# A graph layer's packed slots moved in four held transfers, and one multiply per chunk moved from VectorE to GpSimd

## The chip, the cores and the metric

The kernel runs on one core of a Trainium2 chip. The metric is the device time of one execution in microseconds (us); lower is better. Three timed runs of the kernel before took 541.56, 544.33 and 547.14 us, median 544.33. The profile is of one more execution, which took 538.86 us; its span from the first to the last instruction is 537.0 us. The engines are named as in the profile: PE is TensorE, DVE is VectorE, ACT is ScalarE, POOL is GpSimd, SP is SyncE (which here only issues transfers).

## What is computed

A graph network layer with a residual and a layer norm, on 6250 nodes with 128 features and 100,000 edges that are sorted by destination:

```python
Xs = X[src]
m_data = Xs @ W_data.T + b_data
m_ctrl = Xs @ W_control.T + b_control
msg = jnp.where((edge_types == 0)[:, None], m_data, m_ctrl)
agg = jax.ops.segment_sum(msg, dst, num_segments=X.shape[0])
out = jax.nn.relu(agg + (X @ W_self.T + b_self))
x = _layernorm(x + out, axis=-1)
```

Every node thus sums one of two products per incoming edge, chosen by the edge's type.

## The kernel before

**Messages.** At the start both products are computed for all nodes and kept in SBUF as `m3`, each number split into three bf16 parts (384 columns), 98 blocks of 128 rows (49 blocks of nodes, two products each). A copy goes to a table in memory.

**Windows and groups.** The destination nodes are cut into 39 windows of 160 nodes; an edge list of 22 x 126 edges covers a window. Windows come in groups: one of 1, one of 2, nine of 4 (`GROUPS`). The code has two phases per group.

**ranks** (from L720) prepares a group, long ahead of its use. It finds for each edge its block of source rows, counts edges of a block with matmuls (`rk`, L823 and L864) and gets by a reduction on DVE (`slot`, L869) the edge's slot among 32 slots of that block. For two chunks of the group's edges (12 and 10 of the 22 columns, 48 and 40 edge columns for a group of 4 windows) DVE then takes three large bf16 steps: `hr` (L893, the one-hot of the slot, 126 x 1536 or 126 x 1280 elements), and twice a multiply into `two` (L899): `hr` times the row within the block (`lo1`), and `hr` times the destination within the window (`to1`). Matmuls on PE (`scatter`, L908) put these numbers into the slots (`vt`); three small DVE steps (L923 to L929) turn them into `vs`, which SP writes to memory as `packed` (L935). GpSimd then makes `to_d` from `vs` (L492), picks out edges that found no slot (`pv`, L955 and L957), and a list of these is made by DVE, GpSimd and PE in turn (`fl`, `n8b`, `pos`, `hr` L992, matmuls L1011), gathered from the table by GpSimd (L1034) and copied by SP into `gl` (L1041).

**sums** (from L1048) does the windows of a group. SP reads a window's packed slots (3136 numbers of 2 bytes) and gives them to all 128 partitions, 784 KB, into `rows`, which has two buffers (L1061). One DVE step compares them with the partition number (L1071), which makes `rows` a one-hot matrix of 32 slots by 98 blocks. Two DVE steps make `hot` from `to_d` (L1079), the one-hot of the destination. Then come 25 steps g: stage 1 (L1093, four matmuls side by side) gathers 128 slots' messages into PSUM, ACT or DVE evicts them to `gs` (L485 and L486), stage 2 (L1110 and L1113) adds them into the window's sum `a`. `close` adds the window's own product, the ReLU, the residual and the layer norm; its last step is on GpSimd (L678).

**What sets the order.** `add` does not issue an instruction; it records an operation with an engine, an assumed duration and a due time. `Plan.run` then plays the whole program in assumed time: on each engine it takes, of the operations that are ready, the one with the earliest due time, and the order so found is the order in which instructions are issued to each engine's queue. Every queue runs in order on the chip. Assumed durations on GpSimd come from `pool(cols, rate)`, 0.4 + cols x rate / 1000 us, on DVE from `dve(cols, rate)`, 0.07 + cols x rate / 1000 us; a signal from DVE is booked with 0.14 us and one from GpSimd with 0.15 us. Ranks are due about 80 us ahead of their sums, so their operations come first wherever they are ready. `vp(on_pool, ...)` records a step on GpSimd or on DVE:

```python
def vp(on_pool, due, cols, fn, r, w, rate=1.04, slow=1.0):

    if on_pool:
        return add("POOL", pool(cols, slow), lambda: fn(G), due, r, w)
    return add("DVE", dve(cols, rate), lambda: fn(V), due, r, w)
```

Before the change, `RP` is 1, so that L1061 makes one transfer for a window; its place on the queue follows from the planned end of the matmuls that free the buffer.

Of the kernel before, what the change touches and what calls it, by code (L numbers as in the profile page):

```python
# [21 lines left out]
P = 128  # L22
D = 128
D3 = 3 * D
# [20 lines left out]
R = 32  # L45
# [42 lines left out]

class Op:
    __slots__ = ("alts", "due", "lat", "deps", "after", "left", "ready", "start", "end", "out",  # L90
                 "index", "engine", "slack", "size")

    def __init__(self, alts, due, lat):
        self.alts, self.due, self.lat, self.slack, self.size = alts, due, lat, 0.0, 0
        self.deps, self.after, self.out = [], [], []


class Plan:
# [5 lines left out]
    FROM = 60.0  # L104
    BEGIN, RATE, LAND = 1.2, 0.28, 0.8

    def __init__(self):
        self.ops, self.rings, self.far = [], {}, set()

    def add(self, engine, dur, fn, due, r=(), w=(), lat=0.0, size=0):  # L110
        alts = engine if isinstance(engine, list) else [(engine, dur, fn)]
        op = Op(alts, due, lat)
        op.index, op.size = len(self.ops), size
        kind = [(i[0] if isinstance(i, tuple) else i).name for i in w] or ["out"]
        if engine == "SP" and due > self.FROM:
            op.slack = self.SLACK.get(kind[0], 0.0)
        self.ops.append(op)
        deps = set()
        for items, writes in ((r, False), (w, True)):
            for item in items:  # L120
                b, key = item if isinstance(item, tuple) else (item, None)
                for k, (ws, rs) in b.keys.items():
                    if key is None or k is None or k == key:
                        deps.update(ws)
                        if writes:
                            deps.update(rs)
                if writes and key is None:
                    b.keys = {}
                ws, rs = b.keys.setdefault(key, ([], []))
                if writes:  # L130
                    b.keys[key] = ([op], [])
                else:
                    rs.append(op)
                if not b.users or b.users[-1] is not op:
                    b.users.append(op)
        deps.discard(op)
        op.deps = list(deps)
        return op

    def since(self, op, engine):  # L140
        return op.ready + (0.0 if op.alts[0][0] == engine else self.OTHER)

    def run(self):
# [70 lines left out]
                    offer(o)  # L214
                    o.left = -1
        order.sort(key=lambda x: x[:2])
        for _, _, _, fn in order:
            fn()
        return order


# [45 lines left out]
def sums_over_windows(ctx, tc, x, xt, edges, w, bias, out, total):  # L267
# [4 lines left out]
    work = ctx.enter_context(tc.tile_pool(name="work", bufs=2))  # L272
    ps = ctx.enter_context(tc.tile_pool(name="ps", bufs=1, space=PSUM))
    ctx.enter_context(tc.manual_schedule())
    plan = Plan()
    add = plan.add

    table = dram.tile([NT * P, D3], BF16, name="table")
# [15 lines left out]
    GC = 1.3  # L294
    SPD = 0.45
    AD = 0.45
    RP, RA, RS = 1, 14, 0.9
    GAP, LEAD, LF, SF = -12, 80, .3, .010


# [230 lines left out]
    for q in range(NS):  # L531
# [42 lines left out]
        if q % 2 or q == NS - 1:  # L574
# [2 lines left out]
                tv[:, t0:t1, :], m3.t[:, t0:t1, :]), due + 8, m3_key(q) + m3_key(q - q % 2),  # L577
                [(table_b, q)], size=(ts.stop - t0) * P * D3 * 2)


    def own(o, lhs, n):

# [146 lines left out]
    def ranks(gi, w0, nw, when, late, step, engines):  # L729
# [145 lines left out]
        for ci, (k0, k1) in enumerate(zip(cs, cs[1:])):  # L875
# [22 lines left out]
            for i, f in enumerate((lo1, to1)):  # L898
                tf = lambda e, c=c, s4=s4, v4=v4, i=i, f=f, hr=hr, two=two: e.tensor_tensor(  # L899
                    v4(two.t[:EP, :, i, :]), v4(hr.t),  # L900
                    fl(f)[:, c, None, :].to_broadcast(s4), op=ALU.mult)
                vec(dc, m * R, lambda tf=tf: tf(V), [hr, f], [(two, i)], 0.52)

            def scatter(k0=k0, k1=k1, two=two):
                for k in range(k0, k1):
# [144 lines left out]
    def sums(gi, w0, nw, placed):  # L1050
# [5 lines left out]
        for i in range(nw):  # L1056
            due = T0 + (w0 + i) * TW
            sp = B(work, [P, R, NT], BF16, "rows", 2, R * NT)
            for j in range(RP):
                Q = ("ACT", AD, A) if gi < 3 and i == 0 else ("SP", SPD, S)  # L1060
                add(*Q[:2], lambda i=i, sp=sp, j=j, Q=Q: Q[2].dma_start(  # L1061
                    sp.t[P // RP * j : P // RP * (j + 1)].rearrange("p r c -> p (r c)"),
                    packed[gi, i // 2, (i % 2) * 64 : (i % 2) * 64 + R, :]
                    .rearrange("r c -> (r c)")[None, :].to_broadcast([P // RP, R * NT])),
                    due - RA + RS * j, [(packed_b, gi)], [(sp, ("p", j))],
                    size=P // RP * R * NT * 2)
            cut = 2 if gi < 3 else 1
            half = R // cut
            for q in range(cut):
# [16 lines left out]
            for g in range(NS):  # L1086
                d = due + TW * g / NS
                gp = B(ps, [P, 512], F32, *(("g", 3) if gi < 2 or g % 4 < 3 else ("x", 1)))
                last = g == NS - 1

                def stage1(g=g, gp=gp, sp=sp, last=last):
                    for t in (0, 1) if last else turn(4, D3):
                        T.matmul(gp.t[R * t : R * t + R, :D3], sp.t[:, :, 4 * g + t],  # L1093
                                 m3.t[:, 4 * g + t, :], start=True, stop=True)
                s1.append(add("PE", 0.163, stage1, d, [sp] + m3_key(g), [gp]))
                lag = 2 if gi < 2 else 3
                if g >= lag:
                    s2[g - lag].after.append(s1[g])
                if last:
                    gs = gls[i]  # L1100
                    evict(lambda gs=gs: gs.t[:64], lambda gp=gp: gp.t[:64, :D3], D3, d + 0.3,
                          [gp], [(gs, "t")], LAT)
                else:
                    gs = B(work, [P, D3], BF16, "gs", 6)
                    evict(lambda gs=gs: gs.t, lambda gp=gp: gp.t[:, :D3], D3, d + 0.3, [gp], [gs],
                          LAT)

                def stage2(g=g, gs=gs, a=a, hot2=hot2, last=last):
                    for j in turn(4, D3):
                        T.matmul(a.t[R * j : R * j + R, :D3], hot2.t[:, g, R * j : R * j + R],  # L1110
                                 gs.t, start=g == 0, stop=False, skip_group_check=True)
                    for c, j in enumerate(turn(3, D, [3] * (g == 1))):
                        T.matmul(a.t[R * j : R * j + R, D3:], hot2.t[:, g, P:],  # L1113
                                 gs.t[:, c * D : (c + 1) * D], start=False, stop=g > 0,
                                 skip_group_check=True)
                s2.append(add("PE", 0.204, stage2, d + 0.9, [gs, (hot2, sum(g >= c for c in cuts[1:-1]))], [a]))
                s2[-1].slack = .1
                if g == 12:
                    def own_a(i=i, a=a, xc=xc):
                        own(lambda j, m: a.t[R * j : R * j + R, :D],  # L1120
                            lambda j, m: xc.t[:, i * WN + R * j : i * WN + R * j + R], P)
                    add("PE", 0.28, own_a, d + 1, [xc, w_sb, one3, brows], [a])
            bs = B(work, [P, D], F32, "bs", 5)
            evict(lambda bs=bs: bs.t, lambda a=a: a.t[:, D3:], D, due + TW + 0.8, [a], [bs]).slack = 0.25
            got.append((w0 + i, a, due + TW + 0.8, bs))
        return got

# [264 lines left out]
```

## Time and profile before

| | |
|---|---|
| timed runs, us | 541.56, 544.33, 547.14 |
| profiled execution, us | 538.86 |
| its span, us | 537.0 |
| mean granted TensorE clock | 0.987 |
| bytes moved, MB | 63.03, mean 117 GB/s |
| transfers of packed slots | 36 from SP, 3 from ACT, 784 KB each |
| rate of the 16 DMA engines' busy time from 260 to 460 us | 0.35 |

How to read the lines below. A line of the timeline has the start in us after the span's start, the duration in us, engine, line of the kernel, operation, output from input, and in brackets the idle time of the engine just before it and what ended it. A line of groups has the shape, the count, then the busy time in us, the mean in ns, and the idle time before them. A line of waits has who waited, for whom, then total us, times, and the longest in us. A line of a table by stages has the stage, its length, and for PE, PEld (weight loads), DVE, ACT and POOL the busy time and the number of instructions, then the granted clock, the share of the DMA engines' time and GB/s. "issue" is time in which an engine waited for nothing that the profile shows. A line of the chain has the start, the duration and the work. SPq and POOLq are the queues' own waits and issues.

### The profile page before, as it was taken

To read this page: it belongs to the slowest core of one execution; us is meant where nothing else is said; L and a number is where in the kernel's file an instruction comes from. 1 tells how busy PE (TensorE), PEld (TensorE's weight loads), DVE (VectorE), ACT (ScalarE), POOL (GpSimd) and SP (SyncE) were. 2 spreads that over 40 slices of the span, in tenths; PEclk is the share of its full clock that TensorE was granted. 3 is DMA by queue.
4 is the path that set the end of the run, shared out by engine and by line. 5 is a ranking of instruction groups with operands and counts; after the bars stand their busy time and mean duration, and the time that the engine had idled before them with its cause. 6 is when DMAs were issued, how large, how long until landed. Compare 5 with 4: busy or idle time off the path is not lost.

```text
span 537.0 us, 30923 instructions
## 1 busy us (share of the span) xinstructions
PE 496.3 (92%) x13288; PEld 427.5 (80%) x13288; DVE 434.2 (81%) x1154; ACT 436.0 (81%) x1092; POOL 196.1 (37%) x284
## 2 busy tenths in 40 slices
PE   8999678899999999999998989899899999999991
PEld 5666457799899899989977878888888887899890
DVE  6689798999999999999988979978785796644632
ACT  4687457799898898899888879888887887999991
POOL 1000503501830792564465258375215415402000
PEclk9999899999999999999999999999999999999997
DMA  7576550333343236234324433423332335322300
GB/s 239 194 290 253 170 170 16 110 103 118 90 116 107 78 118 182 76 94 128 100 84 121 137 100 99 137 69 91 99 113 76 95 95 177 114 78 102 121 18 17
DMA packets 44568, 63.03 MB, mean 117 GB/s; under 512 B 18832, under 2 KB 34933, under 8 KB 44405
## 3 DMA queue, kind: packets, MB, share of 16 engines
q1 hardware_dynamic: 41657, 55.90, 32.6%
q0 software_dynamic: 1120, 2.23, 1.8%
q10 hardware_dynamic: 1646, 2.84, 1.5%
q8 instruction: 106, 1.74, 1.3%
q14 instruction: 39, 0.32, 0.2%
HBM read 45.46 MB, written 13.57 MB: 110 GB/s over the span
## 4 chain that ended last, share of the span: by engine, by line
PE 60%; DVE 5%; issue 3%; POOL 2%; ACT 2%; another core or an unknown queue 0%; DVEq 0%; ACTq 0%; POOLq 0%
PE a L1110 22%; PE g L1093 20%; PE x L1093 6%; PE a L1113 4%; PE rk L864 3%; PE vt L908 2%; ACT gs L485 2%; PE a L585 1%; POOL to_d L492 1%; DVE hots L812 1%; PE vt L1011 1%; DVE hot L1079 0%; POOL pv L955 0%; PE rk L823 0%
## 5 line engine op out<-in xcount | busy, mean ns | idle before, releaser
L1110 PE MATMUL a<-gs,hot 128*32 128x384 bf16 x3744 | 359.7, 328 | 1.4 <-ACT gs L485 1.0
L485 ACT CAST gs<-g 128x384 bf16<-128x384 f32 x698 | 303.6, 512 | 56.2 <-PE g L1093 46.1
L1093 PE MATMUL g<-m,rows 128*32 128x384 bf16 x2958 | 302.2, 333 | 8.6 <-DVE rows L1071 3.9
L1093 PEld LDWEIGHTS <-rows 128*32 128x32 bf16 x3822 | 260.0, 134 | 25.7 <-issue 13.2
L1113 PE MATMUL a<-gs,hot 128*32 128x128 bf16 x2808 | 267.4, 220 | 7.1 <-issue 6.9
L1110 PEld LDWEIGHTS <-hot 128*32 128x32 bf16 x3900 | 180.4, 98 | 9.4 <-issue 3.5
L1113 PEld LDWEIGHTS <-hot 128*32 128x32 bf16 x2925 | 152.0, 97 | 19.5 <-issue 10.2
L485 ACT CAST gs<-x 128x384 bf16<-128x384 f32 x212 | 110.0, 519 | 8.4 <-PE x L1093 5.3
L1093 PE MATMUL x<-m,rows 128*32 128x384 bf16 x864 | 94.6, 329 | 1.7 <-ACT gs L485 1.1
L1079 DVE TENSOR_TENSOR hot<-iota_b,to_d 128x1920 bf16<-128x1920 bf16 (+2 forms) x85 | 94.3, 1112 | 0.1
L678 POOL TENSOR_SCALAR xr<-xr,mv,rstd 128x128 f32<-128x128 f32 (+1 forms) x44 | 57.2, 1307 | 42.5 <-DVE rstd L655 39.1
L869 DVE TENSOR_REDUCE slot<-rk 126x8 f32<-126x400 f32 (+2 forms) x99 | 56.1, 567 | 14.7 <-PE rk L864 12.3
L628 DVE TENSOR_REDUCE s<-a 128x128 f32<-128x384 f32 (+1 forms) x40 | 22.0, 551 | 32.2 <-PE a L1113 21.3
L1071 DVE TENSOR_SCALAR rows<-rows,pid 128x3136 bf16<-128x3136 bf16 (+1 forms) x46 | 41.8, 908 | 2.2 <-DMA rows<-packed 2.2
L823 PE MATMUL rk<-hots,later 126*32 126x200 bf16 (+1 forms) x210 | 43.1, 246 | 0.3 <-DVE hots L816 0.3
L864 PE MATMUL rk<-hots,tri 128*32 128x400 bf16 (+1 forms) x388 | 41.2, 334 | 1.5 <-DVE slot L869 1.5
L492 POOL COPY to_d<-vs 32x100 bf16<-32x100 bf16 (+1 forms) x72 | 34.9, 485 | 10.8 <-issue 4.8
L955 POOL TENSOR_SCALAR pv<-slot 126x88 f32<-126x88 bf16 x9 | 10.7, 1188 | 73.3 <-DVE slot L886 73.3
L1034 POOL DMA_INDIRECT sr<-table,at x20 | 23.6, 1178 | 17.5 <-DVE slot L886 11.0
L816 DVE TENSOR_TENSOR hots<-hots,val 126x1200 bf16<-126x1200 bf16 (+3 forms) x42 | 28.0, 672 | 0.0
L812 DVE TENSOR_TENSOR hots<-iota_b,st 126x1200 bf16<-126x1200 bf16 (+3 forms) x42 | 28.0, 675 | 0.1
L864 PEld LDWEIGHTS <-tri 128*32 128x32 bf16 x428 | 20.9, 96 | 6.1 <-issue 4.7
(227 smaller groups left out, 648.7 us busy)
## 6 DMA issues: line engine op xcount, KB each, us to landing
rows<-packed SPq DMA_DIRECT2D x36, 784.0 KB
table<-m SPq DMA_DIRECT2D x12, 768.0 KB
xc<-in_xt SPq DMA_DIRECT2D x9, 320.0 KB
rows<-packed ACTq DMA_DIRECT2D x3, 784.0 KB
xr<-in_x SPq DMA_DIRECT2D x8, 256.0 KB
out<-xr SPq DMA_DIRECT2D x8, 256.0 KB
gl<-sr SPq DMA_DIRECT2D x39, 48.0 KB
rows<-in_xt SPq DMA_DIRECT2D x5, 256.0 KB
```

Of the source, the lines that this page charges most:

```text
L485: [("ACT", act(cols), lambda: A.copy(o(), src())), ("DVE", dve(cols), lambda: V.tensor_copy(o(), src()))], None, None, due, r, w, lat)
L492: "POOL", 0.25 + cols * 0.0014, lambda: G.tensor_copy(o(), src()), due, r, w)
L678: fp = lambda k=k, m=m: G.tensor_scalar(h.t[:m, k, :], h.t[:m, k, :], mv.t[:m, k, 0:1], rstd.t[:m, k : k + 1], op0=ALU.subtract, op1=ALU.mult)
L812: vec(when + 2 + pace * k0, m * NC, lambda k0=k0, k1=k1, hs4=hs4, hp=hp: V.tensor_tensor(hp(), iota1_b.t[:EP, :NC].rearrange("p (c d) -> p ...
L823: T.matmul(cnt.t[3 * R :, :wide], later.t[:EP, R - 1 - k : 2 * R - 1 - k], flat(k, k + 1, EP), start=k < 1, stop=k > KT - 3, skip_group_ch ...
L864: T.matmul(acc.t[R * j : R * j + R, : (k1 - k0) * wide], tri.t[:, R * j : R * j + R], flat(k0, k1, P), start=True, stop=True, skip_group_c ...
L869: vec(due, (k1 - k0) * wide, lambda k0=k0, k1=k1, acc=acc: V.tensor_reduce(slot.t[:, k0:k1, :], acc.t[:EP, : (k1 - k0) * wide].rearrange(" ...
L1071: add("DVE", dve(half * NT, 0.305) + 0.05, lambda sp=sp, rs=rs: V.tensor_scalar(sp.t[:, rs], sp.t[:, rs], pid1.t, None, op0=ALU.is_equal), ...
L1079: lambda i=i, hot2=hot2, s4=s4, c0=c0, c1=c1: V.tensor_tensor(hot2.t[:, c0:c1].rearrange("p g (c d) -> p g c d", d=2), iota1_b.t.rearrange ...
L1093: T.matmul(gp.t[R * t : R * t + R, :D3], sp.t[:, :, 4 * g + t], m3.t[:, 4 * g + t, :], start=True, stop=True)
L1110: T.matmul(a.t[R * j : R * j + R, :D3], hot2.t[:, g, R * j : R * j + R], gs.t, start=g == 0, stop=False, skip_group_check=True)
L1113: T.matmul(a.t[R * j : R * j + R, D3:], hot2.t[:, g, P:], gs.t[:, c * D : (c + 1) * D], start=False, stop=g > 0, skip_group_check=True)
```

## The change

Two things change.

1. The transfer of a window's packed slots. From the fourth group on (32 windows) it becomes four transfers of 32 partitions each, 196 KB. The first is due as before (14 us ahead of the window's due time), the others 0.5 us apart behind it; each of the others is held until stage 1 of the window before has done its step g = 3, 6 or 9: the planner counts this matmul among the transfer's dependencies, and a wait on its signal is added to the transfer. For this, an operation keeps its gate and its instruction, `stage1` returns its last matmul, and `marks` keeps every window's stage-1 operations. The first three groups keep one transfer.

2. The second multiply into `two` (with `to1`) goes to GpSimd from the fourth group on, with an assumed duration of 0.4 us + 2.2 ns a column; in the first three groups it stays on DVE.

```diff
+    def hold(self, op, gate):
+
+        op.gate = gate
+        op.deps.append(gate)
...
-        for _, _, _, fn in order:
-            fn()
+        for _, _, op, fn in order:
+            op.inst = fn()
+            if op.gate is not None:
+                self.tc.add_manual_dep(
+                    op.inst.ins, op.gate.inst.ins.name, mybir.DependencyInfo(
+                        mybir.DependencyClass.Sync, mybir.DependencyReason.SCHED_ONLY),
+                    reason="spread transfers")
...
-    RP, RA, RS = 1, 14, 0.9
+    RP, RA, RS = 4, 14, 0.5
...
-                vec(dc, m * R, lambda tf=tf: tf(V), [hr, f], [(two, i)], 0.52)
+                vp(i == 1 and gi >= 3, dc, m * R, tf, [hr, f], [(two, i)], 0.52, 2.2)
...
-            for j in range(RP):
+            gate = marks[w0 + i - 1] if gi >= 3 else None
+            cut = RP if gate else 1
+            for j in range(cut):
                 Q = ("ACT", AD, A) if gi < 3 and i == 0 else ("SP", SPD, S)
-                add(*Q[:2], lambda i=i, sp=sp, j=j, Q=Q: Q[2].dma_start(
-                    sp.t[P // RP * j : P // RP * (j + 1)].rearrange("p r c -> p (r c)"),
+                op = add(*Q[:2], lambda i=i, sp=sp, j=j, Q=Q, cut=cut: Q[2].dma_start(
+                    sp.t[P // cut * j : P // cut * (j + 1)].rearrange("p r c -> p (r c)"),
                     packed[gi, i // 2, (i % 2) * 64 : (i % 2) * 64 + R, :]
-                    .rearrange("r c -> (r c)")[None, :].to_broadcast([P // RP, R * NT])),
+                    .rearrange("r c -> (r c)")[None, :].to_broadcast([P // cut, R * NT])),
                     due - RA + RS * j, [(packed_b, gi)], [(sp, ("p", j))],
-                    size=P // RP * R * NT * 2)
+                    size=P // cut * R * NT * 2)
+                if j:
+                    plan.hold(op, gate[3 * j])
...
                 def stage1(g=g, gp=gp, sp=sp, last=last):
                     for t in (0, 1) if last else turn(4, D3):
-                        T.matmul(gp.t[R * t : R * t + R, :D3], sp.t[:, :, 4 * g + t],
-                                 m3.t[:, 4 * g + t, :], start=True, stop=True)
+                        mm = T.matmul(gp.t[R * t : R * t + R, :D3], sp.t[:, :, 4 * g + t],
+                                      m3.t[:, 4 * g + t, :], start=True, stop=True)
+                    return mm
...
+            marks.append(s1)
```

Since the planner knows the new durations and waits, the order on all queues is worked out anew.

More of the change, by code (lines that the diff above doesn't have):

```diff
@@ L90 @@
     __slots__ = ("alts", "due", "lat", "deps", "after", "left", "ready", "start", "end", "out",
-                 "index", "engine", "slack", "size")
+                 "index", "engine", "slack", "size", "gate", "inst")
     def __init__(self, alts, due, lat):
@@ L95, in __init__ @@
         self.deps, self.after, self.out = [], [], []
+        self.gate, self.inst = None, None
 class Plan:
@@ L105, with __init__ @@
     BEGIN, RATE, LAND = 1.2, 0.28, 0.8
-    def __init__(self):
+    def __init__(self, tc):
+        self.tc = tc
         self.ops, self.rings, self.far = [], {}, set()
@@ L274, in sums_over_windows @@
     ctx.enter_context(tc.manual_schedule())
-    plan = Plan()
+    plan = Plan(tc)
     add = plan.add
@@ L578, in sums_over_windows @@
                 [(table_b, q)], size=(ts.stop - t0) * P * D3 * 2)
+    marks = []
     def own(o, lhs, n):
```

## The prediction

> **What bounds the kernel now.** I read the page first, then busy time by stage, then what each engine waits for, then single stretches of the timeline.
>
> ```profile
> span 537.0 us, 30923 instructions
> PE 496.3 (92%) x13288; PEld 427.5 (80%) x13288; DVE 434.2 (81%) x1154; ACT 436.0 (81%) x1092; POOL 196.1 (37%) x284
> PE 60%; DVE 5%; issue 3%; POOL 2%; ACT 2%; another core or an unknown queue 0%; DVEq 0%; ACTq 0%; POOLq 0%
> q8 instruction: 106, 1.74, 1.3%
> ```
>
> PE carries 60% of the chain that ended last and "issue" 3%. The table of stages (per stage: PE busy, its instructions, then PEld, DVE, ACT, POOL) says where PE is not full:
>
> ```profile
> 110.00:260.00 150.00, 148.94 (x4477) 136.49 (x4473) 142.75 (x346) 134.45 (x345) 66.45 (x94) 1.00 0.37 114
> 260.00:460.00 200.00, 186.25 (x5508) 165.25 (x5502) 167.04 (x414) 166.37 (x424) 93.99 (x132) 1.00 0.35 104
> 460.00:520.00 60.00, 59.88 (x1765) 53.84 (x1760) 30.30 (x64) 58.48 (x156) 9.22 (x10) 1.00 0.27 89
> ```
>
> From 110 to 260 and from 460 on PE has no room (1.1 and 0.1 us idle). From 260 to 460 it idles 13.75 us: what the change can win lies there. PE's waits from 110 to 520 (in total, times, longest):
>
> ```profile
> PE a L1113 <- issue: 6.9, 8, 2.2
> PE vt L1011 <- DVE hr L992: 2.4, 2, 2.0
> PE g L1093 <- issue: 0.8, 3, 0.3
> PE x L1093 <- issue: 0.5, 1, 0.5
> ```
>
> 8.2 us (6.9 + 0.8 + 0.5) of PE's idle time is "issue": no semaphore held it. Two rows show one such stop, in the middle of a straight run of matmuls; the SP queue's rows and the DMA table (last column GB/s) show what went on:
>
> ```profile
> 347.49 0.22 PE L1113 MATMUL a<-gs,hot 128*32 128x128 bf16 x1
> 349.89 0.23 PE L1113 MATMUL a<-gs,hot 128*32 128x128 bf16 x2 [2.17 <-issue]
> ```
>
> ```profile
> 342.39 0.35 SPq L1061 DMA_DIRECT2D rows<-packed  x1
> 342.80 0.43 SPq L1053 DMA_DIRECT2D xc<-in_xt  x1
> 343.40 0.38 SPq L601 DMA_DIRECT2D xr<-in_x  x1
> ```
>
> ```profile
> 344.50:346.50 2.00, 2.00 (x82) 1.85 (x80) 2.00 (x4) 1.16 (x5) 0.00 (x0) 1.00 0.94 318
> 346.50:347.70 1.20, 1.20 (x36) 0.88 (x28) 1.20 (x2) 1.20 (x5) 0.00 (x0) 1.00 0.99 313
> 347.70:349.90 2.20, 0.03 (x8) 0.01 (x4) 1.26 (x3) 0.45 (x2) 0.00 (x0) 1.00 0.20 51
> ```
>
> The packed slots and what SP issues right behind them saturate the DMA engines until 347.7; PE stops there and comes back 2.2 us later. The instruction queue of the page moved 1.74 MB in 106 packets, 16.4 KB each; PE and PEld ran 26,576 instructions, 251 a packet. So PE lives on pages of about 250 instructions, one per 4.3 us (3,525 instructions in the last 60 us stage are 58.8 per us). A page asked for during a burst of 4 to 5 us comes too late. The chain has two more such stops:
>
> ```profile
> 286.72 1.49 issue
> 385.51 1.45 issue
> ```
>
> The second comes 5.4 us after a transfer of packed slots (380.15, below). This is my reading; no row names the fetch.
>
> **The change, part by part.**
>
> 1. *The transfer in four.* From the fourth group on (32 of 39 windows) the 784 KB of a window become 4 x 196 KB; the first goes as before, the others wait on SP for stage-1 matmuls 3, 6 and 9 of the window before. Removed: the burst. The largest load at once falls from 784 + 320 + 256 KB to 196 + 320 + 256 KB, at some 310 GB/s from 4.4 to 2.5 us, well under the 4.3 that a page lasts. Of the 8.2 us I take off 7.3 (low end 0, if the stops have another cause; high end 8.2).
> [...]
>
> Added: 96 issues on SP of 0.35 us and three waits per window. SP already stands there:
>
> ```profile
> SPq L1061 <- PE g L1093: 187.3, 32, 11.2
> 380.15 0.33 SPq L1061 DMA_DIRECT2D rows<-packed  x1
> 392.20 0.34 SPq L1061 DMA_DIRECT2D rows<-packed  x1
> 386.01 1.03 DVE L1071 TENSOR_SCALAR rows<-rows,pid 128x3136 bf16<-128x3136 bf16 x1
> ```
>
> A window lasts 12.05 us (392.20 - 380.15), so matmul 9 of 25 comes 4.3 us in; with 0.3 us for the issue and, as an estimate, 2.5 us to land (196 KB at 310 GB/s is 0.6; the 1360 KB issued from 342.39 on were through at 347.7, 0.9 us more than the 4.4 they take at 310 GB/s; I allow 1 more), the last quarter is there at 387.3 instead of before 386.01. The compare (1.03 us) can still end 3.8 us before 392.2. Queued behind the waiting SP are the counts of the ranks (past), the list rows (gl), xr and out; the planner knows of the waits and orders SP by them, and for these transfers ranks, matmuls and closing steps would wait. I cost this at 0; if the compare comes after the window's start, PE waits for all that is late, in each of 32 windows.
>
> 2. *The multiply moved to GpSimd.* 16 steps (two chunks in each of 8 groups) leave DVE:
>
> ```profile
> L899 DVE TENSOR_TENSOR two<-hr,to 126x1280 bf16<-126x1280 bf16 x9 | 9.4, 1046 | 0.0
> L899 DVE TENSOR_TENSOR two<-hr,to 126x1536 bf16<-126x1536 bf16 x9 | 8.8, 972 | 0.0
> ```
>
> 8 x (1.05 + 0.97) = 16.1 us of DVE. PE hardly waits for DVE: 2.4 us at L1011 above is the largest, so the gain is between 0 and 2.4; I take 1.
>
> The price on GpSimd: no row has a two-operand step of this size. The nearest are two small ones (ns min/median/max):
>
> ```profile
> L986 POOL TENSOR_TENSOR pos<-iota_f,pos_all x9: 265/266/1248, 98.4 to 450.1; 126x48 bf16<-126x48 f32 x9
> L783 POOL TENSOR_TENSOR pay<-pay,lof x9: 368/495/1461, 55.7 to 355.8; 126x88 f32<-126x88 f32 x9
> L783 POOL TENSOR_TENSOR pay<-pay,lof 126x88 f32<-126x88 f32 x9 | 6.4, 716 | 0.6
> ```
>
> The last row has the mean, 716 ns. From the minima: (368 - 265) / 40 = 2.6 ns an element and 0.14 us fixed; that makes 4.1 us for 1536 elements and 3.5 us for 1280. The maxima come from DVE:
>
> ```profile
> 408.57 1.25 POOL L986 TENSOR_TENSOR pos<-iota_f,pos_all 126x48 bf16<-126x48 f32 x1
> 408.55 1.15 DVE L1079 TENSOR_TENSOR hot<-iota_b,to_d 128x1920 bf16<-128x1920 bf16 x1
> 409.86 0.98 DVE L992 TENSOR_TENSOR hr<-iota_b,pos 126x1536 bf16<-126x1536 bf16 x1 [0.16 <-POOL pos L986]
> ```
>
> While DVE runs one of its bf16 passes GpSimd stands still: 0.27 us of work took 1.25. Over its nine runs L783 takes 1.9 times its minimum (716 to 368).
>
> The planner books 0.4 + 2.2 ns an element, 3.78 and 3.22 us, and puts the scatter matmuls on PE that far behind. PE runs in order, so what GpSimd takes beyond this, PE waits for; PE now comes some 0.7 us after the last weights (392.75 to 393.47 below), of which I count 0.4 as spare. Walk through the tenth group's two chunks:
>
> ```profile
> 388.96 0.96 DVE L893 TENSOR_TENSOR hr<-slot_f,slot 126x1536 bf16<-126x1536 bf16 x1
> 390.94 0.95 DVE L899 TENSOR_TENSOR two<-hr,lo 126x1536 bf16<-126x1536 bf16 x1
> 391.80 0.95 DVE L899 TENSOR_TENSOR two<-hr,to 126x1536 bf16<-126x1536 bf16 x1
> 393.47 0.88 PE vt L908 x48
> 394.58 1.23 DVE L1079 TENSOR_TENSOR hot<-iota_b,to_d 128x2080 bf16<-128x2080 bf16 x1
> 399.69 0.82 DVE L893 TENSOR_TENSOR hr<-slot_f,slot 126x1280 bf16<-126x1280 bf16 x1
> 400.99 0.79 POOL L957 TENSOR_TENSOR pv<-pv,pay 126x88 f32<-126x88 f32 x1
> ```
>
> First chunk: GpSimd could start at 390.0, does 0.9 us until 390.94, little beside lo, 2.7 until the bf16 pass at 394.58, and ends near 395. Booked is 389.92 + 3.78 and 0.29 for two signals, 394.0, with the spare 394.4: 0.6 us late. Second chunk: GpSimd is busy with pv to 401.78, then 3.5 us, end 405.3; booked 400.51 + 3.22 + 0.29, with the spare 404.4: 0.9 late. 1.5 us a group, 8 groups, 12 us. At the planner's 2.2 ns the steps end 0.5 us earlier, 0.1 and 0.4 late, 4 us in all. Slowed as L783 is, 7.8 and 6.7 us long, they are 3.6 and 3.1 late, 54 us; half of that, 27, is my upper bound, since the stretch above shows DVE between its bf16 passes for more than half of the time. The lower bound is 0. Between 4 and 12 I take 5: a slope from 0.10 us of difference is coarse, and DVE has 1 us less to do beside each step. What stands on GpSimd behind the second chunk (the list) comes later too, but of 3.2 us of that the plan knows.
>
> Sum on the profiled execution (538.86 us, span 537.0): -7.3 - 1 + 5 = -3.3, 535.6 us. That execution was faster than all three timed runs (541.56 to 547.14, median 544.33), so I put the difference on the median: **541.0 us**. About 1% (5.4 us) is what a measurement of this kernel can tell from no change.
>
> **The rivals.**
>
> *GpSimd's step is covered.* If it runs at the planner's rate and DVE's bf16 passes fall elsewhere, it ends within what is booked and the spare; -7.3 - 1.7 (between 1 and 2.4), 535.3 us. For: the bare time is nearly the booked one. Against: lo and the pass at 394.58 stand in the stretch above.
>
> *PE stands at the scatter.* Slower: at L908, in order, PE waits for GpSimd's last weights. From 8.3 / 16 = 0.5 us a chunk beyond the spare on, it eats all that is won. At 1.25 us a chunk PE loses 20 us, less 8.3: 556 us. For: where GpSimd's pos is late today, DVE's L992 waits for it and PE for L992 (2.4 us above). Against: the booked time leaves over half of the step covered in any case.
>
> *Another cause of the stops.* If PE isn't short of pages, the held transfers do nothing: -1 + 5, 548.3 us. For: no row names the fetch. Against: the stop at 347.7 begins when the burst ends, and nothing else ends there. [...]
>
> **How the numbers follow.** The forecast (541, own range 535.5 to 546.5) gets 0.45, the covered step 0.25, the standing PE 0.22, the other cause 0.08. Faster by over 1% (under 538.9): 0.25 and 0.10 of the forecast's; within 1%: 0.35 of the forecast's and 0.03 of the last; slower: 0.22 and 0.05. The range, 530 to 555, takes in the covered step with the whole of 8.2 and 2.4 (533.7; the timed runs lie up to 2.8 off their median) and a PE that stands up to 1.2 us beyond the spare at each scatter.
>
> **What would show it.** Right: PE's waits for "issue" from 110 to 520 under 2 us, none over 1; no DMA stretch of 4 us at over 0.9; L899 on POOL at 4 to 6 us; 0 to 1 us of PE waiting at L908 per chunk. Wrong: issue stops that stay (no fetch behind a burst); L899 on POOL at 7 us or more with PE waits at L908 over 15 us in all; DVE waiting for the rows' transfer.

## The result and the profile after

The changed kernel takes 563.01 us (median of 6 runs, 559.68 to 565.84) where the kernel before takes 541.51 us on the same chip: the ratio is 1.040, with a 95% interval of 1.034 to 1.047. It is slower by 4%; the forecast was 541 us and its range ended at 555.

The page of the profiled execution after: the span, the busy times, and the shares of the chain that ended last.

```profile
span 564.3 us, 31221 instructions
PE 501.9 (89%) x13288; PEld 429.4 (76%) x13288; DVE 459.7 (81%) x1147; ACT 434.6 (77%) x1083; POOL 232.4 (41%) x300
PE 51%; DVE 25%; DMA 8%; POOL 6%; issue 5%; ACT 3%; ACTq 0%; SPq 0%; DVEq 0%; POOLq 0%
```

DVE's share of the chain went from 5% to 25%, and DVE is busy for 25.5 us more than before (459.7 against 434.2), though 16.1 us of work were taken off it. So about 41.6 us (25.5 + 16.1) came onto DVE from somewhere. GpSimd's new step is the next row to look at: by source line (durations as minimum, median and maximum in ns), and by form with the mean.

```profile
L913 POOL TENSOR_TENSOR two<-hr,to x16: 2339/2784/2947, 124.1 to 465.4; 126x1536 bf16<-126x1536 bf16 x8, 126x1280 bf16<-126x1280 bf16 x8
```

```profile
L913 DVE TENSOR_TENSOR two<-hr,lo 126x1536 bf16<-126x1536 bf16 x9 | 27.6, 3062 | 0.0
L913 POOL TENSOR_TENSOR two<-hr,to 126x1280 bf16<-126x1280 bf16 x8 | 22.9, 2858 | 0.0
L913 POOL TENSOR_TENSOR two<-hr,to 126x1536 bf16<-126x1536 bf16 x8 | 22.2, 2780 | 54.1 <-DVE hr L907 40.9 <-PE g L1111 7.7 <-PE x L1111 5.6
```

GpSimd's 16 steps take 45.1 us (22.9 + 22.2), 2.8 us each, less than I had priced. But DVE's multiply with lo, 0.95 us before, has a mean of 3.06 us. The timeline of DVE and GpSimd shows why:

```profile
170.20 1.03 DVE L1089 TENSOR_SCALAR rows<-rows,pid 128x3136 bf16<-128x3136 bf16 x1 [3.23 <-DMA rows<-packed]
...
172.20 0.95 DVE L907 TENSOR_TENSOR hr<-slot_f,slot 126x1536 bf16<-126x1536 bf16 x1
173.55 3.34 DVE L913 TENSOR_TENSOR two<-hr,lo 126x1536 bf16<-126x1536 bf16 x1
176.81 0.55 DVE L642 TENSOR_REDUCE s<-a 128x128 f32<-128x384 f32 x1
177.28 0.56 DVE L883 TENSOR_REDUCE slot<-rk 126x8 f32<-126x400 f32 x1
```

```profile
173.30 2.78 POOL L913 TENSOR_TENSOR two<-hr,to 126x1536 bf16<-126x1536 bf16 x1 [5.58 <-PE x L1111]
```

GpSimd begins at 173.30 and runs its bare time, to 176.08. DVE begins lo 0.25 us later, at 173.55, and ends at 176.89: the 2.53 us that GpSimd still needs, and then its own 0.81. The step that began first was served, and the other stood for the whole rest of it. In the second chunk, here that of an earlier group, DVE begins first:

```profile
128.81 0.90 DVE L1097 TENSOR_TENSOR hot<-iota_b,to_d 128x1440 bf16<-128x1440 bf16 x1
...
135.33 0.81 DVE L913 TENSOR_TENSOR two<-hr,lo 126x1280 bf16<-126x1280 bf16 x1
136.86 2.25 DVE L1097 TENSOR_TENSOR hot<-iota_b,to_d 128x1440 bf16<-128x1440 bf16 x1
```

```profile
135.42 2.93 POOL L913 TENSOR_TENSOR two<-hr,to 126x1280 bf16<-126x1280 bf16 x1
```

There lo is undisturbed, GpSimd takes 2.93 us instead of 2.34, and the next bf16 pass of DVE that follows (hot, 0.90 us at 128.81) takes 2.25. In four other chunks the step that stands is a small one in f32, `inside`, 2.0 us instead of 0.24; before and after by form:

```profile
L753 DVE SCALAR_TENSOR_TENSOR inside<-rel,low 126x88 f32<-126x88 f32 x9 | 2.4, 262 | 0.0
```

```profile
L767 DVE SCALAR_TENSOR_TENSOR inside<-rel,low 126x88 f32<-126x88 f32 x9 | 9.6, 1062 | 0.0
```

So it is not bf16 passes alone that are held. Of the 41.6 us, 30 lie beside GpSimd's steps: 18.9 at lo, 7.2 at `inside`, 3.9 at hot. Another 4.4 us are eight evictions of PSUM that the new order gives to DVE instead of ACT (30 against 22). The other 7 us I have not placed.

What is behind DVE's standing is the loop of ranks. The chain that ended last, around the same place:

```profile
165.26 4.75 DMA rows<-packed
170.20 1.03 DVE rows L1089
...
173.55 0.67 DVE two L913
174.32 2.50 issue
176.81 0.55 DVE s L642
177.36 0.49 DVE slot L883
177.89 0.35 PE rk L878 x4
```

The reduction of the ranks (slot, L883) stands behind lo in DVE's order, and PE's next rank matmuls need it. The 2.50 us called "issue" are the time in which lo stands: no semaphore holds it. PE's waits from 110 to 500 us (total, times, longest):

```profile
PE rk L878 <- DVE slot L883: 10.9, 6, 2.1
PE g L1111 <- DVE rows L1089: 3.8, 3, 1.7
PE vt L1025 <- DVE hr L1006: 3.7, 3, 1.9
...
PE a L1132 <- issue: 1.0, 3, 0.4
...
PE g L1111 <- issue: 0.5, 2, 0.3
...
PE a L1129 <- issue: 0.3, 1, 0.3
```

The waits for "issue" did fall, from 8.2 to 1.8 us. In their place stand 10.9 us for slot, which was no row of PE's before, and 3.8 for rows. The row of the stage from 110 to 260 (PE's busy time first) shows it:

```profile
110.00:260.00 150.00, 136.40 (x4020) 123.07 (x4017) 138.37 (x313) 122.47 (x311) 79.80 (x98) 1.00 0.38 99
```

From 110 to 260 PE had 1.1 us idle before and has 13.6 now, in a stage where it did 4477 matmuls and now does 4020.

### The profile page after: what moved, and what is told of

Same layout as the page of the kernel before. It is cut to its first block, busy times and chain, and to the rows that moved or that the text cites. A ratio compares the mean times of both kernels' runs of the same rounds, so it can differ in the third digit from the quotient of the medians.

```text
span 564.3 us, 31221 instructions
## 1 busy us (share of the span) xinstructions
PE 501.9 (89%) x13288; PEld 429.4 (76%) x13288; DVE 459.7 (81%) x1147; ACT 434.6 (77%) x1083; POOL 232.4 (41%) x300
## 4 chain that ended last, share of the span: by engine, by line
PE 51%; DVE 25%; DMA 8%; POOL 6%; issue 5%; ACT 3%; ACTq 0%; SPq 0%; DVEq 0%; POOLq 0%
PE a L1129 16%; PE g L1111 16%; PE x L1111 4%; DVE two L913 4%; DVE hot L1097 4%; DVE slot L883 3%; PE a L1132 3%; POOL to_d L504 3%; DMA rows<-packed 3%; DVE rows L1089 3%; PE rk L878 3%; ACT gs L497 2%; DVE hr L907 2%; PE vt L922 2%; PE g L561 2%
## 5 line engine op out<-in xcount | busy, mean ns | idle before, releaser
L497 ACT CAST gs<-g 128x384 bf16<-128x384 f32 x690 | 299.6, 504 | 75.4 <-PE g L1111 65.8
L1111 PEld LDWEIGHTS <-rows 128*32 128x32 bf16 x3822 | 256.6, 135 | 33.5 <-issue 12.9
L1132 PE MATMUL a<-gs,hot 128*32 128x128 bf16 x2808 | 259.4, 220 | 1.3 <-issue 1.0
L1129 PEld LDWEIGHTS <-hot 128*32 128x32 bf16 x3900 | 172.7, 98 | 8.9 <-issue 3.7
L1132 PEld LDWEIGHTS <-hot 128*32 128x32 bf16 x2925 | 146.0, 97 | 14.0 <-issue 2.9
L497 ACT CAST gs<-x 128x384 bf16<-128x384 f32 x212 | 107.7, 508 | 14.9 <-PE x L1111 13.8
L1097 DVE TENSOR_TENSOR hot<-iota_b,to_d 128x1920 bf16<-128x1920 bf16 (+2 forms) x85 | 98.2, 1160 | 0.1
L1111 PE MATMUL x<-m,rows 128*32 128x384 bf16 x864 | 91.7, 331 | 1.4 <-ACT gs L497 1.1
L883 DVE TENSOR_REDUCE slot<-rk 126x8 f32<-126x400 f32 (+2 forms) x99 | 56.1, 567 | 14.1 <-PE rk L878 11.5
L692 POOL TENSOR_SCALAR xr<-xr,mv,rstd 128x128 f32<-128x128 f32 (+1 forms) x44 | 50.7, 1160 | 40.7 <-DVE rstd L669 40.4
L913 POOL TENSOR_TENSOR two<-hr,to 126x1536 bf16<-126x1536 bf16 (+1 forms) x16 | 45.1, 2819 | 54.1 <-DVE hr L907 40.9
L878 PE MATMUL rk<-hots,tri 128*32 128x400 bf16 (+1 forms) x388 | 40.5, 337 | 13.4 <-DVE slot L883 12.4
L878 PEld LDWEIGHTS <-tri 128*32 128x32 bf16 x428 | 21.3, 96 | 21.7 <-issue 20.2
L913 DVE TENSOR_TENSOR two<-hr,lo 126x1536 bf16<-126x1536 bf16 (+4 forms) x21 | 36.5, 1738 | 0.0
```

Of the source, the lines that this page charges most:

```text
L497: [("ACT", act(cols), lambda: A.copy(o(), src())), ("DVE", dve(cols), lambda: V.tensor_copy(o(), src()))], None, None, due, r, w, lat)
L692: fp = lambda k=k, m=m: G.tensor_scalar(h.t[:m, k, :], h.t[:m, k, :], mv.t[:m, k, 0:1], rstd.t[:m, k : k + 1], op0=ALU.subtract, op1=ALU.mult)
L878: T.matmul(acc.t[R * j : R * j + R, : (k1 - k0) * wide], tri.t[:, R * j : R * j + R], flat(k0, k1, P), start=True, stop=True, skip_group_c ...
L883: vec(due, (k1 - k0) * wide, lambda k0=k0, k1=k1, acc=acc: V.tensor_reduce(slot.t[:, k0:k1, :], acc.t[:EP, : (k1 - k0) * wide].rearrange(" ...
L1097: lambda i=i, hot2=hot2, s4=s4, c0=c0, c1=c1: V.tensor_tensor(hot2.t[:, c0:c1].rearrange("p g (c d) -> p g c d", d=2), iota1_b.t.rearrange ...
L1111: mm = T.matmul(gp.t[R * t : R * t + R, :D3], sp.t[:, :, 4 * g + t], m3.t[:, 4 * g + t, :], start=True, stop=True)
```

## The experiments

Each result is the ratio to the kernel before on the same chip, with its 95% interval in brackets. Each profile is of one execution.

Theory A (the expectations call it the port theory; the runs show who stands and for how long, not what in the chip makes it so): GpSimd's step and DVE's passes over SBUF exclude each other, and what DVE loses reaches PE by slot. Rivals: the planner's new order costs the time; the transfers in quarters do; PE waits for GpSimd's result.

**Each half alone.** First only GpSimd's step, the transfers whole:

```diff
-    RP, RA, RS = 4, 14, 0.5
+    RP, RA, RS = 1, 14, 0.5
```

> Only the multiply goes to GpSimd; one transfer of 784 KB per window as before. Port theory (a two-operand step on GpSimd and one on DVE exclude each other for the whole length of the one that began first): DVE's multiply with lo still takes 3.3 us beside the 2.8 us step, PE waits some 2 us for the ranks' slots in each of 8 groups, time 552 to 558. Transfer theory (the held quarters land late and that is the loss): time within 1% of before, 536 to 547, though the multiply with lo may be long.

Measured: 1.031 [1.025, 1.037], and the same wait of PE:

```profile
PE rk L878 <- DVE slot L883: 10.4, 8, 2.1
```

Then only the held quarters, both multiplies on DVE:

```diff
-                vp(i == 1 and gi >= 3, dc, m * R, tf, [hr, f], [(two, i)], 0.52, 2.2)
+                vec(dc, m * R, lambda tf=tf: tf(V), [hr, f], [(two, i)], 0.52)
```

> Only the transfers change: four quarters, held at matmuls 3, 6 and 9; both multiplies on DVE. Port theory: the loss of the whole change is mostly gone, time 538 to 548, the rows' compare still waits for its quarters (some 8 us in all). Transfer theory: 555 or more. If PE's unexplained stops were late instruction pages, its waits for issue at the last matmuls of stage 2 (6.9 us before) stay at 1 us as in the changed kernel.

Measured: 1.012 [1.006, 1.018]. The two halves, 17.5 and 6.1 us, add up to the 21.5 us of the whole within their uncertainty.

**GpSimd's multiply in four pieces**, each a quarter of the columns:

```diff
+                    for c0 in range(0, m, cn):
...
+                        add("POOL", pool(m * R, 2.2) / 4, tq, dc, [hr, f], [(two, 1)])
```

> As with GpSimd only (one transfer of 784 KB), but GpSimd's multiply is cut into four steps of a quarter of the columns. Port theory: each step holds DVE for 0.7 us at most, the multiply with lo takes 1.4 to 1.7 us instead of 3.3, the time falls by 5 to 10 us against the uncut step. If DVE is held for another reason (the tile that both read), the multiply with lo stays near 3 us and the time too.

Measured: 1.019 [1.013, 1.025]. By form:

```profile
L919 POOL TENSOR_TENSOR two<-hr,to 126x384 bf16<-126x384 bf16 x32 | 36.5, 1170 | 54.2 <-DVE hr L907 40.7 <-PE g L1121 13.5
L919 POOL TENSOR_TENSOR two<-hr,to 126x320 bf16<-126x320 bf16 x32 | 30.3, 974 | 0.0
...
L913 DVE TENSOR_TENSOR two<-hr,lo 126x1536 bf16<-126x1536 bf16 x9 | 11.3, 1254 | 0.0
```

DVE's lo now stands for no more than a part of one piece (mean 1.25 us, longest 1.50), and PE's wait for slot falls from 10.4 to 3.1 us. GpSimd's steps grew together to 66.8 us (36.5 + 30.3), and still the kernel is faster than with one long step: it is DVE's standing that costs.

**The step kept, its length taken away, the order unchanged.** This run has the instructions of the first one in the same order on every engine; GpSimd's multiply takes 32 columns instead of 1536 or 1280. It leaves out the factor with the destination for the other columns, where `hr` stands in its place.

```diff
-                v4(hr.t),
+                v4(two.t[:EP, :, 1, :] if gi >= 3 else hr.t),
...
+                if gi >= 3:
+                    take = 1 if i else m
```

> The kernel with GpSimd's step and whole transfers (ratio 1.031, DVE's lo at 3.3 us in most chunks), in the same order of instructions on every engine, but GpSimd's multiply takes 32 of the 1536 (1280) elements. Left out: the factor with the destination for the others; hr stands in its place in the weights, so the sums of the wrong lists come out. Port theory (the two steps exclude each other for as long as GpSimd's lasts): lo is back at 0.8 to 1.0 us, PE's wait for slot at L878 under 5 us in all, time within 1.5% of before. Rival (the planner's new order costs the time, not the collision): ratio still 1.025 to 1.035.

Measured: 1.001 [0.997, 1.005], PE's wait for slot 0.9 us. GpSimd's step and lo:

```profile
L918 DVE TENSOR_TENSOR two<-two,lo x16: 806/916/960, 122.6 to 433.1; 126x1536 bf16<-126x1536 bf16 x8, 126x1280 bf16<-126x1280 bf16 x8
L918 POOL TENSOR_TENSOR two<-two,to x16: 235/239/900, 123.7 to 434.1; 126x32 bf16<-126x32 bf16 x16
```

This settles the first half: with the order as it is and the long step gone, all of the 3.1% is gone. The order is thus not its cause. The short step also ends earlier, so this run alone doesn't exclude that PE waits for GpSimd's result. The other profiles do: PE's waits of the changed kernel and of the first run have no row for `two` from GpSimd, and with the four pieces, whose steps are longer in all, that row is 0.3 us. The run also shows that the best that the move could have brought in this order is nothing: here DVE is rid of the 16 us and nearly nobody does them, and the time is that of before.

**GpSimd later, and with one operand.** Three runs tried to move or shrink the collision. In the first only the planner was told that the step needs lo:

```diff
+                vp(i == 1 and gi >= 3, dc, m * R, tf, [hr, f] + [(two, 0)] * (i == 1 and gi >= 3), [(two, i)], 0.52, 2.2)
```

> GpSimd only (one transfer), but GpSimd's multiply begins when DVE's multiply with lo is done. Port theory: the multiply with lo takes 0.95 us again, the collision moves to what DVE does next with two operands in SBUF (hot, 1.2 us, takes up to 3), time 548 to 557, between the uncut step (+17 us) and none. If it is not the overlap of the two that costs, the time stays at 556 to 562.

Measured: 1.050 [1.044, 1.056]. It tested nothing but another order: on the chip GpSimd still began as soon as hr was there, and lo of 1536 columns still took 2.8 us in the mean. The next run put a real wait on lo there, and has the order of this one on DVE, GpSimd and SP:

```diff
+                if i == 1 and gi >= 3:
+                    plan.hold(op, lo_op)
+                lo_op = op
```

> What the run in which GpSimd's multiply was to begin after DVE's multiply with lo was meant to be: there only the planner knew of it and on the chip GpSimd began with the one-hot as before; here GpSimd waits for lo on the chip. Port theory: lo takes 0.95 us in every chunk, the collision moves to the next step of DVE with two operands in SBUF, 1 to 2.5 us longer in some chunks; the time is 1 to 2.5% over before, under the uncut step's 3.1%.

Measured: 1.048 [1.044, 1.052], more than expected. All lo are back at 0.95 and 0.82 us, and the next pass over SBUF stands in their place:

```profile
178.53 2.78 POOL L913 TENSOR_TENSOR two<-hr,to 126x1536 bf16<-126x1536 bf16 x1 [6.08 <-DVE two L913]
```

```profile
178.78 3.36 DVE L1092 TENSOR_SCALAR rows<-rows,pid 128x3136 bf16<-128x3136 bf16 x1
```

That pass is the compare of the rows, with one tensor operand: 3.36 us instead of 1.03, once more the 2.53 us that GpSimd still needs and 0.83 of its own. The next reduction of the ranks stands behind it, and PE's waits for slot are 8.7 us. In this order PE also waits 2.1 us for GpSimd's weights. Why this order costs more than the first run's 3.1%, with the collision at lo or behind it, is open. In the third, GpSimd's step has one operand, in the first run's order; it copies `hr` and leaves out the factor with the destination:

```diff
+                    tf = lambda e, hr=hr, two=two: e.tensor_single_scalar(
+                        two.t[:EP, :, 1, :], hr.t, 1.0, op=ALU.mult)
```

> GpSimd only (one transfer), but its step reads one operand: it copies the one-hot of the slot times 1.0 and leaves out the factor with the destination, so the sums are those of wrong lists. If only a two-operand step on GpSimd holds DVE, the multiply with lo takes 0.95 us again and the time is 536 to 545 on a chip where before is 535 to 542. If any GpSimd step on SBUF holds DVE's two-operand steps, lo takes 0.8 us and what is left of GpSimd's step (1.5 to 2 us), 2.3 to 2.8 in all, and the time is 1 to 2% over before.

Measured: 1.047 [1.043, 1.051]. The step got longer with one operand, not shorter, and lo stands as before:

```profile
L917 POOL TENSOR_SCALAR two<-hr 126x1536 bf16<-126x1536 bf16 x8 | 33.4, 4174 | 54.1 <-DVE hr L907 29.2 <-PE g L1114 24.9
L917 POOL TENSOR_SCALAR two<-hr 126x1280 bf16<-126x1280 bf16 x8 | 29.8, 3727 | 0.6
...
L913 DVE TENSOR_TENSOR two<-hr,lo 126x1536 bf16<-126x1536 bf16 x9 | 27.7, 3074 | 0.0
```

So on neither side is a second tensor operand needed for the collision. With the run above this gives three lengths of GpSimd's step in one order: a short one costs nothing, 44.5 us in all cost 3.1%, 63.2 us (33.4 + 29.8) cost 4.7%.

**The quarters.** Four runs on what the transfers in parts cost. Without the waits:

```diff
-                if j:
-                    plan.hold(op, gate[3 * j])
```

> Four quarters at the same due times, but none is held; both multiplies on DVE. If late instruction pages come from the size of one transfer, the waits for issue stay at 1 us and the time is 533 to 541; if they come from the bytes in flight at once, the stops are back (6 us or more) and the time is that of before, 539 to 545. If the hold costs nothing, this is no faster than the held quarters.

Measured: 1.013 [1.008, 1.018], as with the waits; PE's waits for "issue" are 7.8 us without the waits and 4.1 with them. Two halves, the second held:

```diff
-    RP, RA, RS = 4, 14, 0.5
+    RP, RA, RS = 2, 14, 0.5
...
-                    plan.hold(op, gate[3 * j])
+                    plan.hold(op, gate[5 * j])
```

> Transfers alone, two halves of 392 KB, the second held at matmul 5 of the window before; both multiplies on DVE. If stops come from bytes in flight, PE's waits for issue fall to 2 to 4 us; packets of 64 partitions take 0.30 to 0.35 us; time 538 to 546.

Measured: 1.009 [1.006, 1.013], with 6.3 us of waits for "issue", more than expected. Then the order of before, and the four quarters issued back to back; and the same with quarters of the columns, so that each goes to all 128 partitions:

```diff
+                    for k in range(cut):
+                        Q[2].dma_start(
+                            sp.t[P // cut * k : P // cut * (k + 1)].rearrange("p r c -> p (r c)"),
```

> The kernel before with its order kept: where it issued one transfer of 784 KB, from the fourth group on it issues four of 196 KB one behind the other. If quarters by themselves cost (each takes the DMA engines longer, 0.37 to 0.40 us a packet against 0.29), the time is that of the unheld quarters, 546 to 552, and the compare waits for them 6 us or more; if the new order was the cost, the time is within 0.5% of before. Unexplained stops of PE: 6 us or more in either case, as the bytes in flight are the same.

```diff
+                            sp.t[:, h * k : h * (k + 1)].rearrange("p r c -> p (r c)"),
```

> The kernel before with its order kept; each window's transfer is cut in four along the columns, 8 of the 32 slots each, to all 128 partitions. If the quarters of 32 partitions cost because they reach few partitions at a time, this costs nothing, 0 to 0.5% over before or a little under it; if four transfers instead of one are the cost (issues on SP, pieces under way at the same time), it is 1% over before like the quarters by partitions.

Measured: 1.011 [1.008, 1.015] and 1.017 [1.014, 1.021], with 4.2 and 10.8 us of waits for "issue". The first of these holds nothing and yet has no more of them than the held quarters; I had expected 6 us or more. So that the holds are what lessens the stops is not shown. DVE's waits for the rows from 110 to 545, in the kernel before, with quarters of the partitions, and with quarters of the columns:

```profile
DVE rows L1071 <- DMA rows<-packed: 2.2, 3, 1.5
```

```profile
DVE rows L1074 <- DMA rows<-packed: 14.3, 13, 1.9
```

```profile
DVE rows L1075 <- DMA rows<-packed: 8.0, 10, 2.1
```

So cutting the transfer costs 1% or more without any new order, and it comes later to the compare. The stage of 260 to 460 has the DMA engines busier for the same bytes where the partitions are cut (0.46 against 0.35 before, at 106 and 104 GB/s):

```profile
260.00:460.00 200.00, 188.86 (x5623) 170.10 (x5615) 169.47 (x417) 170.91 (x435) 93.86 (x135) 0.99 0.46 106
```

By columns the share is 0.36, and that run is no faster; the busier engines are not the whole cause, and the rest stays open. One run changed the order alone, by a planner's cost (0.5 us for an issue on SP):

```diff
-    SPD = 0.45
+    SPD = 0.5
```

> The kernel before with one assumed duration in the planner changed (an issue on SP 0.5 instead of 0.45 us): no work is added or moved, only the order on the queues is worked out anew. It gives the size of what a new order alone can do. If the loss of the transfer part (+1.2 to 1.3%, held or not) is the new order, this kernel may be off by about as much, 537 to 549; if it stays within 0.4% of before, the loss of the transfer part must come from the quarters themselves.

Measured: 1.012 [1.007, 1.018]. A new order by itself can cost as much as the quarters do, so the 1.2% of the held quarters can't be parted cleanly into cuts and order.

**What PE's "issue" stops are.** The first attempt doubled the bytes of the slots:

```diff
+                def twice(i=i, sp=sp, Q=Q, n=2 if gi >= 3 else 1):
```

> The kernel before with its order kept; from the fourth group on each window's packed slots are moved twice, one transfer of 784 KB behind the other with the same data. If PE's unexplained stops are instruction pages that come late behind the bytes in flight, the waits for issue grow from 8 us to 16 us or more, many of them over 1 us, and the time by 8 to 25 us. If the stops have another cause, they stay at 6 to 10 us, and only the compare's wait for its transfer grows.

Measured: 1.133 [1.127, 1.139], and the stops did not grow (3.6 us). But DVE waited 62.5 us for the slots and PE 26.7 for slot, so PE hardly ran without a break; that this hid the stops is likely, not shown. The granted clock of this profile was 0.94, against 0.987 before. The next run adds bytes for which nobody waits, and its control only the issues:

```diff
+                        Q[2].dma_start(spare[w, :n], one.to_broadcast([n, R * NT]))
```

> The kernel before with its order; behind each 784 KB transfer of packed slots from the fourth group on, SP issues another 784 KB into a spare region of HBM that nobody reads. Unlike the run with the slots twice, no compare waits for these bytes. Theory of late instruction pages: each burst lasts 2.5 us longer, PE's waits for issue between 110 and 500 us rise from 8 to 16 us or more, ratio 1.015 or more. Rival (the stops have another cause): they stay at 5 to 11 us, and what time is lost shows as waits for other transfers.

> As the run with the spare 784 KB, with 6 KB in their place: the price of 32 more issues on SP alone. Both theories: issue stops of 4 to 12 us, time within 1% of before; if it is slower by more, the issue and not the bytes is what costs in the run with the spare bytes, and in the quarters.

Measured: 1.072 [1.063, 1.082] with the bytes, 0.995 [0.991, 0.998] with the issues alone. PE's waits for "issue" with the bytes:

```profile
PE a L1118 <- issue: 11.9, 8, 2.6
PE a L1115 <- issue: 7.4, 6, 2.1
PE g L1098 <- issue: 4.1, 2, 2.3
PE x L1098 <- issue: 2.8, 1, 2.8
...
PE rk L865 <- issue: 1.1, 1, 1.1
```

and in the control:

```profile
PE a L1118 <- issue: 3.1, 4, 1.1
...
PE a L1115 <- issue: 1.5, 1, 1.5
...
PE g L1098 <- issue: 0.2, 1, 0.2
```

With 0.5 for a short one (L586), 27.8 against 4.8 us. One of these stops by microsecond (PE busy first, DMA share and GB/s last):

```profile
217.00:218.00 1.00, 1.00 (x40) 0.98 (x32) 1.00 (x2) 0.86 (x3) 0.00 (x0) 1.00 0.96 340
218.00:219.00 1.00, 0.66 (x20) 0.40 (x12) 1.00 (x2) 0.98 (x3) 0.00 (x0) 1.00 1.07 303
219.00:220.00 1.00, 0.00 (x0) 0.00 (x0) 0.12 (x1) 0.26 (x1) 0.00 (x0) 1.00 0.47 93
```

The DMA engines are full from 214 to 219 (a share of 0.96 to 1.07 in each microsecond); after 4.7 us of it PE stops for 1.88 us, and no semaphore holds it. More bytes in flight made more stops here: that is shown, since the other profiles in which no transfer is held have 2.5 to 12.2 us of them and this one 27.8. That the stops of the kernel before have the same cause is likely. That what comes late are pages of instructions is still an inference; no row names them.

**A shorter burst with the slots whole.** In the order of before but for a few rows, the group's x (xc, 320 KB) is held until stage-1 matmul 8, or 5, of the window before:

```diff
+        op = add("SP", SPD, lambda: S.dma_start(xc.t, xt[:, w0 * WN : (w0 + nw) * WN]),
...
+        if gi >= 3:
+            plan.hold(op, marks[w0 - 1][8])
```

> The kernel before (whole transfers of packed slots, both multiplies on DVE, nearly its order) with one wait: from the fourth group on, the group's 320 KB of x (xc) waits on SP for stage-1 matmul 8 of the window before, so that it leaves the burst of the packed slots. Theory of bytes (issue stops come from long bursts): PE's issue stops between 110 and 500 us fall from 8 to 5 us or less, ratio 0.990 to 0.998. Rival (what queues behind the wait on SP costs as much as it wins): ratio 1.000 to 1.015, with waits of DVE for rows or of PE for xc or hots.

> As the run with xc held at matmul 8, held at matmul 5: the wait ends earlier, so less queues behind it, and the 784 KB (2.5 us at 310 GB/s) have just landed. Theory of bytes: as there, issue stops of 6 us or less, ratio 0.990 to 0.999. Rival: 1.000 to 1.010.

Measured: 0.999 [0.995, 1.003] and 1.000 [0.996, 1.003], with stops of 4.4 and 6.2 us in their profiles. Whole transfers that nothing holds had 2.5 to 12.2, so a drop of the stops isn't shown; the time stayed the same. No version that does the work beats before by as much as 1%; the 0.5% of the run with the 6 KB issues has no explanation here.

## Why the prediction was wrong

**The step that failed** is in item 2: "16 steps leave DVE", 16.1 us, "so the gain is between 0 and 2.4; I take 1". It took DVE's own steps to be as long beside GpSimd as without it. They are not: DVE was busy for 25.5 us more, not for 16.1 less, and 30 us of it are time in which its steps stood beside GpSimd's. I had the exclusion in front of me, and read it in one direction alone: "While DVE runs one of its bf16 passes GpSimd stands still." It held both ways here, for whichever began first: lo took 3.34 us for 0.95, GpSimd's step 2.93 for 2.34. My walk through a chunk had GpSimd do "little beside lo"; GpSimd starts with hr, 0.25 us ahead of lo, and it was lo that did little. A quoted pair of rows gave a hint: of the steps that I moved, the one with 1280 columns took longer (1046 ns) than the one with 1536 (972 ns), though it has less to do. In the trace before, all nine steps of that row ran beside a step of GpSimd. One of them began while the `pv` of 400.99 to 401.78 that the prediction shows still ran:

```profile
401.41 1.06 DVE L899 TENSOR_TENSOR two<-hr,to 126x1280 bf16<-126x1280 bf16 x1
```

Where DVE came second, the timeline after shows 3.34 us for 0.95; the reductions of ranks, which read PSUM, kept their 0.56 us. What in the chip holds the two apart no row shows, and which of DVE's other steps are held is told here by the rows alone.

**The +5 us at the scatter** did not come. GpSimd's step takes 2.8 us for 1536 columns where I had 4.1 (1.7 ns a column, not 2.6), less than the 3.78 that the planner books, and PE's largest waits have none for it (in three of the other runs it is 1.0 to 2.3 us). So the price of the step was too high, and the place of the damage wrong: not L908 behind GpSimd, but the rank matmuls (L878) behind DVE's slot, 10.9 us there alone. The upper bound had a slip as well: a second chunk of 6.7 us behind `pv` would end 4.1 us late, not 3.1, which makes the 27 us some 30; nothing else changes by it.

**The -7.3 us for the stops** was half right. Of the reading, the part on bytes held (more bytes in flight make more stops), and the stops fell by 6.4 us in the one profile after; how much of this the holds did is open, since quarters without a hold had 4.2 us of them, and whole transfers, in the run where only the planner was told of lo, 2.5. No time came of it: with the held quarters alone the kernel is 1.2% slower, and with xc held and the slots whole the time stayed the same. The +0 for the quarters' landing failed: I had the last one land 2.5 us after its issue, with room for the compare. On the chain above a quarter took 4.75 us (165.26), and DVE stood 3.23 us ahead of that compare; PE's waits for rows come to 3.8 us.

**The rivals.** "PE stands at the scatter" had the sign and, at 556 us, nearly the size; its mechanism, PE behind GpSimd's last weights, is refuted: that wait has no row. Of "another cause of the stops" the spare bytes refute that bytes have no part in them; whether pages come late stays open, and the page that lasts 4.3 us is an estimate from the packets of q8. What I lacked was a rival in which GpSimd slows DVE; by the bare 2.8 us it would have read up to 40 us of DVE (16 times 2.5), of which a DVE that is 81% busy passes on a part. The trace has 30 us, and GpSimd's step alone shows 17.5 us at the end.

## What to carry to other kernels

A step moved from DVE to GpSimd can take DVE's time all the same if DVE has large passes from SBUF to SBUF to do meanwhile, as here, where lo took 3.34 us instead of 0.95 beside a step of 2.78: count the step's length on GpSimd as time in which such a pass may stand, and ask who waits for what comes behind it. Before moving work off an engine, ask what the best case is worth: here a run in which the work was nearly left out gained nothing (1.001). A single row that is slower than its size says can be a collision already in the trace, as it was here (1046 ns for 1280 columns, 972 for 1536), and is worth a look before more of the same is added.

## What was not expected of the hardware

- GpSimd's multiply of a bf16 tensor by a constant (one operand, 126x1536) took 4.17 us in the mean, its product of two tensors of that size 2.78 us. The shortest of 1280 columns are 3.44 and 2.34 us.
- What GpSimd's step held on DVE: bf16 products of two tensors (3.34 instead of 0.95 us), the bf16 compare of rows with one tensor operand (3.36 instead of 1.03), and a small f32 step with two tensors (`inside`, 2.05 instead of 0.24). What it did not hold: the reductions (0.56 us) and evictions (0.55) that read PSUM, and the MAX8 of `pv` (L977, 0.16 us), which reads f32 from SBUF.
- One 784 KB transfer to 128 partitions in four costs 1.1 to 1.7% of this kernel, while 32 more issues of 6 KB cost nothing (0.995).
- Behind a burst of about 5 us at a DMA share of 0.96 to 1.07, PE, DVE and ACT were nearly idle at once: from 219 to 220 in the rows above they are busy for 0, 0.12 and 0.26 us. PE's stop there, 1.88 us, has no releaser in the trace; DVE's longest wait for a transfer of xr in that run is 1.8 us.
